# A graph-attention layer on one NeuronCore: rows led by their own column take x from the residual's tile instead of from the gather, blocks 4 to 23

## The chip, the cores and the metric

One core of a Trainium2 chip. The metric is device microseconds of one execution, the median of the runs. A profile is one execution, recorded by the hardware profiler; its span runs from the first to the last instruction.

## The reference

```
ht    = (h @ W) per head                 # h = x: 4096 x 512, W: 512 x (4 x 512)
e     = leaky_relu(src_i + dst_j) + adj  # adj: 4096 x 4096
att   = softmax(e, axis=-1)
gnn   = mean over heads of att @ ht
out   = layernorm(x + gnn, axis=-1)
```

Entries of `adj` are zero or random up to 1e9, and every diagonal entry is non-zero. A row's largest entry exceeds the next one so far that the softmax is one at that column and zero elsewhere. For such a row the layer is: find the column of the row's maximum, take that row of x, multiply it by the mean of the heads' weights, add the row's own x, normalise. The kernel does this, bounds the gap between the two largest entries, and has a general path (`general`) for rows where the bound fails; the data never need it.

In this data the row's own diagonal entry is the largest in 325 of 4,096 rows; in blocks 4 to 23 in 204 of 2,560.

## The kernel before, in words

The 4,096 rows are cut into 32 blocks of 128. Row p·32 + ib of the matrices belongs to block ib and sits in partition p. `leading_rows` is one loop over steps t = 0 to 31 (L432) with a tail behind it. The whole runs under a manual schedule (L55): each engine executes its instructions in the order in which the code emits them, and waits where an operand is not ready.

A block travels through the loop over several steps:

- SyncE's queue loads the block's 2 MB of `adj` five steps ahead (`load_adj`, L119), into six buffers in turn. x comes in larger pieces into `hold`, a tile that keeps all 32 blocks' x and later their outputs (`load_x`, L126; the table `x_at`, L427, says at which step which blocks). The second half of `hold` first holds the weights.
- Step t = ib: VectorE takes maxima over short segments of each row (`segment_maxima`, L180), the largest of them and its place (`find_segment`, L187 and L189). GpSimd computes the segment's number (L196) and fetches just that segment of each row by an indirect DMA (`fetch_segment`, L200, tile `lead`), then the segment's first column (L207, `start`).
- Step ib + 2: VectorE finds the place within the segment (L223, `within`), GpSimd adds it to `start` (L225, `col`) and gathers 128 rows of x by an indirect DMA into a tile `y` (`gather_rows`, L211; four buffers).
- Step ib + 3: TensorE turns y (L238), ScalarE copies the turned rows to SBUF (L240, `yt`), TensorE adds the block's own x through a product with the identity (`residual`, L246) and the four products with the mean weights (L253).
- Step ib + 4: ScalarE takes sum and squares of the result (`stats`, L275 and L277) and the norm of the block's own x (`row_norm`, L260).
- Every even step from 6: GpSimd turns two blocks' sums into factors (`rstd`, L280 to L282) and ScalarE, at the end of that step, writes the two blocks' outputs into `hold` (`finish`, L286). These are the blocks t - 6 and t - 5.

So in step t ScalarE's list is: the copy of one turned piece of W (steps 1 to 14), the copy of the turned rows of block t - 3, stats and row norm of block t - 4, and in even steps the two finishes. GpSimd's list is: column and gather of block t - 2, in even steps the statistics, then row, fetch and start of block t. The column is found between the two halves of step t's maxima on VectorE.

Until step 15 TensorE also turns W and forms the heads' vectors. Blocks 24 to 31 go a slightly different way, with the own x added later; the outputs are stored at the end, behind all loads in SyncE's queue.

Of the kernel before, what the change touches and what calls it, by code (L numbers as in the profile page):

```python
# [9 lines left out]
F32 = mybir.dt.float32  # L10
U32 = mybir.dt.uint32
I32 = mybir.dt.int32
AF = mybir.ActivationFunctionType
OP = mybir.AluOpType
# [6 lines left out]
P = 128  # L21
# [3 lines left out]
E_LAST = 64  # L25
EARLY = 18
LAST = 4


@with_exitstack  # L30
def gat_resnorm_kernel(
# [29 lines left out]
    any_bad = keep.tile([1, 1], I32, name="any_bad")  # L61

    leading_rows(tc, x, adj, W, a, out, ident, v, n_bad, any_bad)

    flag = nc.values_load(any_bad[0:1, 0:1], min_val=0, max_val=N)
# [5 lines left out]
def leading_rows(ctx, tc, x, adj, W, a, out, ident, v, n_bad, any_bad):  # L71
# [8 lines left out]
    nc = tc.nc  # L80
    N, D = x.shape
    H = a.shape[0]
    KB, NB = D // P, N // P
    AHEAD = 5
    Q = 4
# [4 lines left out]
    once = ctx.enter_context(tc.tile_pool(name="once", bufs=1))  # L90
    adj_pool = ctx.enter_context(tc.tile_pool(name="adj_pool", bufs=AHEAD + 1))
    y_pool = ctx.enter_context(tc.tile_pool(name="y_pool", bufs=4))
    lead_pool = ctx.enter_context(tc.tile_pool(name="lead_pool", bufs=1))
    LEADS = (8, 8, LAST)
    small = ctx.enter_context(tc.tile_pool(name="small", bufs=5))
# [3 lines left out]
    adj_rows = adj.rearrange("(p nb) m -> nb p m", nb=NB)  # L99
    spans = ((E_EARLY, 0, EARLY), (E, EARLY, NB - LAST), (E_LAST, NB - LAST, NB))  # L100
    adj_segs = {e: adj.rearrange("n (s e) -> (n s) e", e=e) for e, _, _ in spans}
# [6 lines left out]
    hold = once.tile([P, NB, D], F32, name="hold")  # L108
# [48 lines left out]
    nc.gpsimd.memset(power, -0.5)  # L157
    eps = once.tile([P, 1], F32, name="eps")
    nc.gpsimd.memset(eps, EPS)

    top = once.tile([P, NB, 8], F32, name="top")
    inner = once.tile([P, NB, 8], F32, name="inner")
# [45 lines left out]

    def gather_rows(ib, col):
        y = y_t[ib] = y_pool.tile([P, D], F32, name="y")  # L210
        nc.gpsimd.indirect_dma_start(  # L211
            out=y, out_offset=None, in_=x,
            in_offset=bass.IndirectOffsetOnAxis(ap=col[:, :1], axis=0),
        )
# [4 lines left out]
    def find_column(ib):  # L219
        if ib < BEHIND:  # L220
            find_inner(ib)
        within = small.tile([P, 8], U32, name="within")
        nc.vector.max_index(within, top[:, ib, :], lead_of[ib])  # L223
        col = small.tile([P, 1], U32, name="col")
        nc.gpsimd.tensor_tensor(col, at_of.pop(ib), within[:, 0:1], op=OP.add)  # L225
        gather_rows(ib, col)

    def find_column_in_row(ib):

        col = small.tile([P, 8], U32, name="col")  # L230
        nc.vector.max_index(col, top[:, ib, :], adj_t[ib])
        gather_rows(ib, col)
# [191 lines left out]
        nc.vector.tensor_reduce(total, pg, axis=AX.X, op=OP.add)  # L424
        nc.vector.tensor_scalar(any_bad, total, -1.0, float(N), op0=OP.mult, op1=OP.add)

    x_at = {Q - 1: (Q, 2 * Q), 3 * Q - 1: (3 * Q, Q), 4 * Q - 1: (4 * Q, 2 * Q)}  # L427
    vectors = [(kb, h) for kb in range(KB) for h in range(H)]
    vectors_at = {t: 2 if t < 3 else 1 for t in range(1, 15)}
    COLUMN, PROJECT, STATS, FINISH = 2, 3, 4, 6  # L430
# [1 line left out]
    for t in range(NB):  # L432
# [29 lines left out]
        ib = t - PROJECT  # L462
# [244 lines left out]
```

## Time and profile before

| | |
|---|---|
| median of 3 runs | 235.18 us (234.89 to 349.29) |
| span of the profiled execution | 233.4 us |
| TensorE, VectorE, ScalarE, GpSimd busy | 86%, 82%, 48%, 43% |
| moved by DMA | 97.12 MB, mean 416 GB/s |
| of which by GpSimd's queue (segments and gathered rows) | 8.84 MB |
| gathers of x | 32, 0.96 us each on GpSimd |

The span stands 1.8 us under the median; what lies around it is not in the profile. PE is TensorE's matmuls, PEld its weight loads, DVE is VectorE, ACT ScalarE, POOL GpSimd, SP SyncE. A row of the timeline has the start, the duration, the engine, the line of the kernel, the operation, the tiles (out<-in), and in brackets the idle time before it with what ended it. A row of the groups has the busy time, the mean of one in ns, and the idle time before. A row of the waits has the total, the number of times and the longest.

### The profile page before, as it was taken

The numbers are of one execution on the slowest core, as the hardware profiler recorded it, in microseconds if no ns is written. First come the engines' busy times: TensorE is split into PE (matmuls) and PEld (weight loads), VectorE is DVE, ScalarE is ACT, GpSimd is POOL, SyncE is SP. The second block draws the span as 40 slices with busy tenths as digits, with TensorE's granted clock in tenths as the row PEclk, the third lists the DMA queues.
The fourth block names the chain that finished last, engine by engine and source line by source line (L and its number), as shares of the span: only waits on it lengthen the run. The fifth ranks groups of instructions, "written<-read, shape, count | busy, mean of one in ns | idle before, by whom it ended". The sixth has DMA issues, their size and how long they took to land.

```text
span 233.4 us, 2484 instructions
## 1 busy us (share of the span) xinstructions
PE 199.9 (86%) x683; PEld 105.3 (45%) x683; DVE 191.3 (82%) x300; ACT 111.8 (48%) x267; POOL 100.7 (43%) x215
## 2 busy tenths in 40 slices
PE   0069995999999999999999779879998977999980
PEld 0034644646565555665645244334443433444460
DVE  0548299689929999999788995999999999998881
ACT  2001223014474757575767455545664644188561
POOL 2020234414524464644543452647464564548300
PEclk9999999579999999999999979999999999999997
DMA  6999999999999999999999999999999999999995
GB/s 237 423 432 428 428 438 426 415 439 436 422 421 437 423 431 425 431 419 428 430 430 428 432 423 432 423 430 421 426 433 420 426 423 426 412 424 420 421 414 213
DMA packets 12257, 97.12 MB, mean 416 GB/s; under 512 B 1992, under 2 KB 2440, under 8 KB 6480
## 3 DMA queue, kind: packets, MB, share of 16 engines
q1 hardware_dynamic: 8640, 88.08, 89.1%
q0 software_dynamic: 3584, 8.84, 9.6%
q8 instruction: 6, 0.10, 0.2%
q14 instruction: 11, 0.09, 0.1%
q10 hardware_dynamic: 16, 0.02, 0.0%
HBM read 88.54 MB, written 8.39 MB: 415 GB/s over the span
## 4 chain that ended last, share of the span: by engine, by line
DMA 64%; DVE 21%; PE 11%; SPq 1%; issue 1%; ACT 0%; DVEq 0%
DMA adj_t<-in_adj_dram 53%; DVE seg L180 17%; DMA hold<-in_x_dram 11%; PE o L253 6%; PE o L295 2%; DVE at L189 1%; PE tp L238 1%; DVE top L187 1%; PE o L246 1%; DVE within L223 1%; SPq L130 1%; PE o L291 0%; SPq L124 0%; DVE inner L217 0%; ACT hold L335 0%
## 5 line engine op out<-in xcount | busy, mean ns | idle before, releaser
L180 DVE TENSOR_REDUCE seg<-adj_t 128x128 f32<-128x2048 f32 (+3 forms) x66 | 145.5, 2208 | 28.5 <-DMA adj_t<-in_adj_dram 28.2
L253 PE MATMUL o<-w_sum,yt 128*128 128x512 f32 x248 | 117.6, 616 | 0.7 <-ACT yt L240 0.7
L253 PEld LDWEIGHTS o<-w_sum,yt 128*128 128x128 f32 x248 | 45.6, 196 | 55.2 <-issue 43.9
L240 ACT COPY yt<-tp 128x512 f32<-128x512 f32 x32 | 18.8, 588 | 43.9 <-PE tp L238 43.8
L200 POOL DMA_INDIRECT lead<-in_adj_dram,row x32 | 32.3, 1008 | 14.6 <-POOL row L196 14.6
L211 POOL DMA_INDIRECT y<-in_x_dram,col x32 | 30.9, 964 | 15.4 <-POOL col L225 15.1
L238 PE MATMUL tp<-ident,y 128*128 128x128 f32 x128 | 22.1, 296 | 10.2 <-DMA y<-in_x_dram,col 10.1
L246 PE MATMUL o<-hold,ident 128*128 128x512 f32 x52 | 28.5, 634 | 1.7 <-DMA hold<-in_x_dram 1.7
L343 PE MATMUL o<-hold,ident 128*128 128x512 f32 x32 | 17.3, 696 | 13.6 <-DMA hold<-in_L_gnn_W_dram 13.6
L238 PEld LDWEIGHTS tp<-ident,y 128*128 128x128 f32 x128 | 18.5, 209 | 22.8 <-issue 20.5
L361 ACT COPY wt<-tp 128x512 f32<-128x512 f32 x16 | 9.2, 587 | 38.2 <-PE tp L359 38.2
L196 POOL TENSOR_TENSOR row<-at,first 128x1 uint32<-128x1 uint32 x32 | 6.1, 190 | 43.6 <-DVE at L189 43.6
L367 PEld LDWEIGHTS pv<-at_d,wt 128*128 128x128 f32 x128 | 17.2, 200 | 7.4 <-ACT wt L361 3.7
L260 ACT ACTIVATE sq<-hold 128x512 f32<-128x512 f32 x32 | 19.8, 620 | 0.0
L225 POOL TENSOR_TENSOR col<-start,within 128x1 uint32<-128x1 uint32 x31 | 5.9, 190 | 32.2 <-DVE within L223 32.2
L286 ACT ACTIVATE hold<-o,nm,sd 128x512 f32<-128x512 f32 x24 | 17.2, 771 | 0.0
L277 ACT ACTIVATE sq<-o,nm 128x512 f32<-128x512 f32 x24 | 16.5, 687 | 0.8
L343 PEld LDWEIGHTS o<-hold,ident 128*128 128x128 f32 x32 | 6.9, 225 | 21.5 <-issue 21.5
L367 PE MATMUL pv<-at_d,wt 128*128 128x2 f32 x128 | 16.0, 249 | 0.6 <-ACT wt L361 0.6
L344 ACT ACTIVATE w_sum<-o 128x512 f32<-128x512 f32 x4 | 2.4, 598 | 27.5 <-PE o L343 27.5
L275 ACT ACTIVATE sq<-o 128x512 f32<-128x512 f32 x24 | 14.5, 606 | 0.0
L187 DVE MAX8 top<-seg 128x8 f32<-128x256 f32 (+2 forms) x32 | 11.6, 362 | 1.1
(86 smaller groups left out, 140.0 us busy)
## 6 DMA issues: line engine op xcount, KB each, us to landing
adj_t<-in_adj_dram SPq DMA_DIRECT2D x28, 2048.0 KB, 30.8
adj_t<-in_adj_dram SPq DMA_DIRECT2D x6, 1024.0 KB, 28.1
hold<-in_L_gnn_W_dram SPq DMA_DIRECT2D x2, 2048.0 KB, 16.4
hold<-in_x_dram SPq DMA_DIRECT2D x2, 2048.0 KB, 37.6
out_dram<-hold SPq DMA_DIRECT2D x4, 1024.0 KB, 16.1
out_dram<-hold SPq DMA_DIRECT2D x7, 512.0 KB, 14.4
hold<-in_x_dram SPq DMA_DIRECT2D x3, 1024.0 KB
adj_t<-in_adj_dram SPq DMA_DIRECT2D x4, 512.0 KB, 19.8
```

What stands on the lines that cost most here:

```text
L180: nc.vector.tensor_reduce(seg_of[ib][:, ts(k, N // e // n)], adj_t[ib][:, ts(k, N // n)].rearrange("p (s e) -> p s e", e=e), axis=AX.X, op ...
L200: nc.gpsimd.indirect_dma_start(out=lead, out_offset=None, in_=adj_segs[e], in_offset=bass.IndirectOffsetOnAxis(ap=row[:, :1], axis=0),)
L211: nc.gpsimd.indirect_dma_start(out=y, out_offset=None, in_=x, in_offset=bass.IndirectOffsetOnAxis(ap=col[:, :1], axis=0),)
L238: nc.tensor.transpose(tp[:, kb, :], y[:, ds(kb, P, KB)], ident)
L240: nc.scalar.copy(yt, tp)
L246: nc.tensor.matmul(o_ps[ib], ident, hold[:, ib, :], start=start, stop=False)
L253: nc.tensor.matmul(o_ps[ib], yt_of[ib][:, kb, :], w_sum[:, kb, :], start=(start and kb == 0), stop=(kb == KB - 1),)
L260: nc.scalar.activation(sq, hold[:, ib, :], AF.Square, accum_out=xx[:, ib : ib + 1])
L277: nc.scalar.activation(sq, o, AF.Square, bias=nm[:, i], accum_out=sd[:, i])
L286: nc.scalar.activation(hold[:, ib, :], o_ps.pop(ib), AF.Identity, bias=nm[:, i], scale=sd[:, i])
L343: nc.tensor.matmul(o, ident, hold[:, w_at + kb * H + h, :], start=(h == 0), stop=(h == H - 1))
L367: nc.tensor.matmul(pv[:, kb, h : 2 * H : H], wt[:, k, :], at_d[:, k, h : 2 * H : H], start=(k == 0), stop=(k == KB - 1),)
```

## The change

For blocks 4 to 23, GpSimd computes three more things from the column of each row: `same` (1 where the column is the row's own number, else 0), `away` (8192 there, else 0), and `there`, their sum with the column. ScalarE writes the block's own x, from `hold`, times `same` into the tile y: own rows where they lead, zeros elsewhere. The gather then runs with `there`: an index beyond the last row is skipped, so those rows of y keep what ScalarE wrote, and the others are overwritten. Since ScalarE now needs the block's x at step ib + 2 instead of TensorE at step ib + 3, three x loads are moved two steps forward.

```diff
+SKIP = 8192
+OWN = range(4, 24)
...
+    numbers = once.tile([P, NB], I32, name="numbers")
+    nc.gpsimd.iota(numbers, pattern=[[1, NB]], base=0, channel_multiplier=NB)
+    own = once.tile([P, NB], F32, name="own")
+    nc.gpsimd.tensor_copy(own, numbers)
...
     def gather_rows(ib, col):
         y = y_t[ib] = y_pool.tile([P, D], F32, name="y")
+        if ib in OWN:
+            same = small.tile([P, 1], F32, name="same")
+            nc.gpsimd.tensor_scalar(same, col, own[:, ib : ib + 1], None, op0=OP.is_equal)
+            away = small.tile([P, 1], U32, name="away")
+            nc.gpsimd.tensor_scalar(
+                away, col, own[:, ib : ib + 1], float(SKIP), op0=OP.is_equal, op1=OP.mult
+            )
+            there = small.tile([P, 1], U32, name="there")
+            nc.gpsimd.tensor_tensor(there, col, away, op=OP.add)
+            nc.scalar.activation(y, hold[:, ib, :], AF.Copy, scale=same)
+            nc.gpsimd.indirect_dma_start(
+                out=y, out_offset=None, in_=x,
+                in_offset=bass.IndirectOffsetOnAxis(ap=there[:, :1], axis=0),
+                bounds_check=N - 1, oob_is_err=False,
+            )
+            return
...
-    x_at = {Q - 1: (Q, 2 * Q), 3 * Q - 1: (3 * Q, Q), 4 * Q - 1: (4 * Q, 2 * Q)}
+    x_at = {1: (Q, 2 * Q), 3 * Q - 3: (3 * Q, Q), 4 * Q - 3: (4 * Q, 2 * Q)}
```

Q is 4: the pieces for blocks 4 to 11, 12 to 15 and 16 to 23 are loaded in steps 1, 9 and 13 instead of 3, 11 and 15, each ahead of that step's load of `adj`.

## The prediction

> **What bounds the kernel now.** I read the page first (shares, slices, queues, chain), then the waits, then the timeline of one block.
>
> ```profile
> span 233.4 us, 2484 instructions
> ...
> PE 199.9 (86%) x683; PEld 105.3 (45%) x683; DVE 191.3 (82%) x300; ACT 111.8 (48%) x267; POOL 100.7 (43%) x215
> ...
> DMA  6999999999999999999999999999999999999995
> ...
> DMA packets 12257, 97.12 MB, mean 416 GB/s; under 512 B 1992, under 2 KB 2440, under 8 KB 6480
> ...
> DMA 64%; DVE 21%; PE 11%; SPq 1%; issue 1%; ACT 0%; DVEq 0%
> ```
>
> The DMA engines are full from the second slice to the last but one, and 64% of the chain is DMA: 97.12 MB at 416 GB/s fill the span. But VectorE (82%) and TensorE (86%) stand close behind, so a delay on either that lasts to the last blocks ends in the time. Who waits:
>
> ```profile
> DVE seg L180 <- DMA adj_t<-in_adj_dram: 28.2, 11, 8.7
> ...
> PE tp L238 <- DMA y<-in_x_dram,col: 10.1, 10, 2.7
> ...
> L211 POOL DMA_INDIRECT y<-in_x_dram,col x32: 962/962/969, 31.1 to 214.6; - x32
> ...
> DMA to landing us min/median/max: 6.2/7.8/9.5
> ```
>
> TensorE waits ten times for gathered rows: there, y arrives just as PE wants it. The gather that the change edits takes 7.8 us (median) from issue to landing. It has no slack in the second half of the stage, and I look at one block of it. Counted from the first issue at 31.1 us, the gather at 162.78 below is block 21's, the turn at 159.71 block 19's, the turn at 170.67 block 21's.
>
> ```profile
> 158.38 0.19 POOL L280 TENSOR_SCALAR sd<-sd 128x2 f32<-128x2 f32 x1
> 158.66 0.72 POOL L281 TENSOR_TENSOR sd<-sd,power 128x2 f32<-128x2 f32 x1
> ...
> 159.71 0.72 PE L238 MATMUL tp<-ident,y 128*128 128x128 f32 x4
> ...
> 160.47 0.59 ACT L240 COPY yt<-tp 128x512 f32<-128x512 f32 x1 [2.49 <-PE tp L238]
> 160.95 0.60 ACT L275 ACTIVATE sq<-o 128x512 f32<-128x512 f32 x1
> ...
> 161.78 0.19 DVE L223 FIND_INDEX8 within<-top,lead 128x8 uint32<-128x32 f32 x1
> ...
> 162.05 0.19 POOL L225 TENSOR_TENSOR col<-start,within 128x1 uint32<-128x1 uint32 x1 [0.42 <-DVE within L223]
> ...
> 162.78 0.97 POOL L211 DMA_INDIRECT y<-in_x_dram,col  x1 [0.54 <-POOL col L225]
> ...
> 162.97 1.43 ACT L286 ACTIVATE hold<-o,nm,sd 128x512 f32<-128x512 f32 x2
> ...
> 165.29 0.72 PE L238 MATMUL tp<-ident,y 128*128 128x128 f32 x4 [0.49 <-DMA y<-in_x_dram,col]
> ...
> 168.46 0.19 ACT L260 ACTIVATION_READ_ACCUMULATOR sq<-hold 128x1 f32 x1
> ...
> 170.67 0.72 PE L238 MATMUL tp<-ident,y 128*128 128x128 f32 x4 [0.28 <-DMA y<-in_x_dram,col]
> ```
>
> Today the gather of block 21 needs only VectorE (within, then col). It is issued while ScalarE is still in the work of loop step 22: the copy of block 19's turned rows, stats and row norm of block 18, two finishes. Gather and ScalarE do not know of each other. Issue to landing to turn is 162.78 + 7.8 + 0.1 = 170.67.
>
> **The change, part by part.** *Bytes.* In the reference's data 204 of the 2,560 rows of blocks 4 to 23 are led by their own column. At 2 KB each that is 0.42 MB of 97.12 MB, at 416 GB/s 1.0 us of DMA work. It counts only if the DMA still sets the end.
>
> *Set-up.* One iota and one copy of 128x32 on GpSimd before any gather: two short instructions, like the 0.19 us ones above, while GpSimd has nothing due until the first maxima. Nothing; without that cover some 0.4 us.
>
> *Three GpSimd operations a block* (same, away, there), 128x1 each. The pair at 158.38 and 158.66 gives 0.28 us from one start to the next, so 0.84 us: the gather could go at 162.24 + 0.84 + 0.54 = 163.62. They lie inside the wait told next; without it they cost 0.84 us a block.
>
> *The x loads, two steps earlier.* The same 2, 1 and 2 MB pass two adjacency loads each in SP's queue. Their cost today is seen as a wait of VectorE:
>
> ```profile
> 69.15 2.29 DVE L180 TENSOR_REDUCE seg<-adj_t 128x128 f32<-128x2048 f32 x1 [4.03 <-DMA adj_t<-in_adj_dram]
> ```
>
> That wait comes two steps sooner. The bytes do not grow, and x is there when ScalarE wants it, since the distance to the need stays the same. Zero; if it fell on a gather without slack, at most those 4.0 us once.
>
> *The write of y by ScalarE, and the wait for it.* This is the dear part. The order on each engine is the order of emission. The write stands at the head of step t on ScalarE, behind everything of step t-1; for block 21 behind the finishes, which end at 162.97 + 1.43 = 164.40. The write itself is not in this trace. Nearest rows:
>
> ```profile
> L286 ACT ACTIVATE hold<-adj_t,nm,sd 128x512 f32<-128x512 f32 x4 | 3.1, 805 | 0.0
> ...
> L275 ACT ACTIVATE sq<-adj_t 128x512 f32<-128x512 f32 x3 | 1.9, 627 | 0.0
> ```
>
> Between 0.63 (fixed scale) and 0.81 us (scale and bias per partition, same memory); with one per-partition operand I take 0.72. GpSimd then issues the gather between 0.1 us (the step from engine to engine: within ends at 161.97, col starts at 162.05) and 0.54 us (its gap ahead of a gather) later; I take 0.3, as part of that gap can pass during the wait. The gather goes at 164.40 + 0.72 + 0.30 = 165.42, not 162.78. It lands 7.8 us later, and PE turns block 21 at 173.35 instead of 170.67.
>
> ScalarE's own wait for same costs nothing here: same is known near 162.24 + 0.28, before ScalarE gets there. Were it ahead, the copy of the next turned rows, for which TensorE waits, would queue behind.
>
> The late gather alone would be a shift of 2.7 us. But **it closes a ring**: turn of b-2, its copy, ScalarE's work behind that, write of y(b), gather, landing, turn of b. One round is 4.69 (159.71 to 164.40) + 0.72 + 0.30 + 7.8 + 0.13 = 13.64 us for two blocks. For an even b there are no finishes ahead: 168.46 + 0.19 - 165.29 = 3.36 in place of 4.69, a round of 12.3. TensorE takes blocks in order, so the odd ring sets 13.64 for two: 6.8 us a block. Now it is 5.5 here (159.71 to 165.29 to 170.67). The ring starts with block 3, whose gather is untouched, and its last gather with the write is that of block 23:
>
> ```profile
> 63.30 0.65 PE L238 MATMUL tp<-ident,y 128*128 128x128 f32 x4
> ...
> 181.90 0.72 PE L238 MATMUL tp<-ident,y 128*128 128x128 f32 x4 [0.45 <-DMA y<-in_x_dram,col]
> ```
>
> Ten rounds, blocks 3, 5, ... 23: 63.30 + 136.4 = 199.7 against 181.90, **17.8 us late on TensorE**. Bounds: 0.1 or 0.54 for the hand-over give 15.8 or 20.2; a landing of 8.2 and 0.54 some 24; one of 6.2, the shortest in the trace, 1.8.
>
> *Behind the waiting gather* on GpSimd stand the step's statistics and the next segment's fetch, so VectorE gets its segments late too:
>
> ```profile
> 176.35 0.19 POOL L196 TENSOR_TENSOR row<-at,first 128x1 uint32<-128x1 uint32 x1 [1.29 <-DVE at L189]
> 177.05 0.96 POOL L200 DMA_INDIRECT lead<-in_adj_dram,row  x1 [0.51 <-POOL row L196]
> ...
> 183.88 0.18 DVE L223 FIND_INDEX8 within<-top,lead 128x8 uint32<-128x32 f32 x1
> ...
> DMA to landing us min/median/max: 5.2/6.1/7.9
> ```
>
> Block 25's segment is fetched after block 23's gather: 199.7 - 7.9 = 191.8, plus 0.97 and 0.70 (row to fetch), 193.5, landing 6.1 later at 199.6, for a search that now runs at 183.88: **15.7 us late on VectorE**. Can the rest of the program win it back? What is left to wait for after 182 us:
>
> ```profile
> PE tp L238 <- DMA y<-in_x_dram,col: 2.3, 3, 1.3
> ...
> DVE seg L180 <- DMA adj_t<-in_adj_dram: 0.4, 2, 0.2
> ```
>
> VectorE has 0.4 us to give and TensorE 2.3, so VectorE ends about 15.3 and TensorE at least 15.5 late. I take 15.5. The 1.0 us of bytes is not credited: the DMA would run dry before the end.
>
> *Sum.* The span of 233.4 us lies 1.8 us under the median of 235.18 us. 233.4 + 15.5 + 1.8 = 250.7 us.
>
> **A rule against this.** The Trainium skill (DMA: Bandwidth & Descriptors, section Anatomy of one DMA — SWDGE (gpsimd) path) fits a transfer from this queue as 2.0 us plus its bytes at 436 GB/s, an estimate of 2.6 us for a gather of 256 KB. The trace does not agree: 7.8 us at the median, 6.2 at the least, with the engines full. By the rule a round would be 8.4 us, no lag would gather, and the sum would be 1.0 us under today.
>
> **The rivals.** *Short flight (the other side).* With 8% of the rows gone, and the DMA less full as the ring slows the loads, the landing could come sooner. The ring stops mattering when a round fits two blocks at their mean pace, (181.90 - 63.30) / 10 = 11.9 us, so from a landing of 7.8 - (13.64 - 11.9) = 6.0 us down. Then only the bytes are left: 235.2 - 1.0 = 234.2 us. Against it: no gather of the trace landed under 6.2 us, and the adjacency loads keep the engines full until the lag has eaten their queue. The rule above falls under this case.
>
> *A shift, not a round.* If lateness did not feed back, the end moves by one delay, 2.7 us at most: 237.9 us. For it: y has slack in the first half, where TensorE waits less. Against it: ScalarE's work ahead of the write starts with a copy that needs the turn two blocks before.
>
> *Starved loads.* If segment fetches land behind the gathers in the one software queue (8.2 us where 7.8 was taken, with 0.54 for the hand-over), VectorE lags some 24 us, its tiles come free late, and the load queue runs dry: 259 us.
>
> *The skipped rows still move.* If an index past the bound still costs a packet, the 1.0 us is not saved. Since it was not credited, the time stays 251 us; the DMA bytes tell.
>
> **How the numbers follow.** Forecast, ring with a lag near 15.5 us: 0.69, own range 244 to 257. Short flight 0.08, shift 0.07, starved loads 0.08, rows still moving 0.05, and 0.03 for a gain that I see no case for. Within 2% (4.7 us, about what a measurement of this kernel can tell from no change) are short flight and shift: 0.15. Slower are the forecast, starved loads and moving rows: 0.82. Faster: 0.03. The range leaves out the two mild cases and reaches down to a ring with landings of some 6.5 us, 63.30 + 123.4 - 181.90 = 4.8 late, 240; up to the starved case, 259.
>
> **What would show it.** A new group of 20 ScalarE writes of y near 0.72 us. GpSimd's gather idle before it, released by that write and not by col, 2 to 3 us after col in the early blocks of the stage. Turns two blocks apart by 13 to 14 us in blocks 5 to 23, ScalarE never waiting long there; waits of the segment search for lead where now there is 0.2 us; DMA slices under 9 after some 190 us. DMA bytes lower by 0.42 MB. I am wrong if the turns keep 11 to 12 us per pair: then either the landings got shorter than 6.5 us or ScalarE reaches the write before the column is known. If the gathers are late but the end is not, then TensorE or VectorE had room that the waits do not show.

## The result, and the profile after

The changed kernel takes 256.69 us (median of 4 runs, 255.66 to 257.2) against 235.09 us before: a ratio of 1.0915, 95% interval 1.0887 to 1.0943, so 21.6 us slower. The 235.09 us are the median of four runs, one more than in the table above, and one of them, at 349.29 us, was a slow run that the ratio leaves out. The forecast was 250.7 us in a range of 240 to 259. The profiled run of the changed kernel took 257.2 us with a span of 255.6.

The page of the changed kernel, its shares, slices and chain:

```profile
span 255.6 us, 2625 instructions
...
PE 209.1 (82%) x683; PEld 109.3 (43%) x683; DVE 191.7 (75%) x300; ACT 125.0 (49%) x287; POOL 118.9 (47%) x277
...
PEclk9999996599976999977999997999999979999999
DMA  6999999999999999999999999998999999971225
GB/s 255 427 434 427 435 419 430 434 425 438 419 431 428 426 422 440 423 435 422 433 424 433 424 431 424 407 389 348 374 352 407 410 320 417 424 288 53 78 110 225
...
DMA 45%; PE 32%; ACT 14%; issue 5%; POOL 1%; DVE 0%; SPq 0%; POOLq 0%
```

VectorE does the same work (191.7 us, 191.3 before) in a longer span. The DMA is no longer full to the end: its rate falls from slice 26 on, and in the last four slices its engines are busy for one to five tenths of the time. ScalarE, which had no share of the chain, now has 14%. 96.72 MB were moved instead of 97.12, and GpSimd's queue alone moved 8.42 instead of 8.84: the skip does what it says. The waits of the changed kernel:

```profile
POOL y L227 <- ACT y L226: 43.0, 18, 5.4
...
PE tp L260 <- DMA y<-in_x_dram,there: 23.0, 14, 3.8
DVE inner L239 <- DMA lead<-in_adj_dram,row: 22.8, 13, 3.2
```

The first line is new: 18 of the 20 gathers are put down as waiting for ScalarE's write of y, 43 us in all. TensorE's wait for y has more than doubled (10.1 us before), and VectorE, which hardly waited for segments (0.2 us), waits 22.8 us for them. The new groups of instructions:

```profile
L226 ACT ACTIVATE y<-hold,same 128x512 f32<-128x512 f32 x20 | 14.4, 719 | 2.3 <-POOL same L219 2.2
...
L227 POOL DMA_INDIRECT y<-in_x_dram,there x20 | 22.4, 1121 | 45.0 <-ACT y L226 43.0 <-PE tp L381 2.0
```

ScalarE itself waits only 2.2 us for `same`. It is late, not held up. One round of the ring, blocks 19 to 21, in the timeline:

```profile
180.12 0.72 PE L260 MATMUL tp<-ident,y 128*128 128x128 f32 x4 [1.16 <-DMA y<-in_x_dram,there]
...
180.88 0.59 ACT L262 COPY yt<-tp 128x512 f32<-128x512 f32 x1 [3.04 <-PE tp L260]
...
183.38 1.44 ACT L308 ACTIVATE hold<-o,nm,sd 128x512 f32<-128x512 f32 x2
...
183.81 0.19 POOL L225 TENSOR_TENSOR there<-col,away 128x1 uint32<-128x1 uint32 x1
...
184.71 0.72 ACT L226 ACTIVATE y<-hold,same 128x512 f32<-128x512 f32 x1
...
186.21 1.12 POOL L227 DMA_INDIRECT y<-in_x_dram,there  x1 [2.20 <-ACT y L226]
...
187.83 0.97 POOL L206 DMA_INDIRECT lead<-in_adj_dram,row  x1 [0.27 <-POOL row L202]
...
193.15 0.72 PE L260 MATMUL tp<-ident,y 128*128 128x128 f32 x4 [1.88 <-DMA y<-in_x_dram,there]
```

The rows to gather are known at 184.00 (`there`). ScalarE copies block 19's turned rows, does its other work, finishes two blocks until 184.82, and only then writes y. The gather follows 0.78 us behind the write (185.43 to 186.21), the segment fetch behind the gather, and TensorE turns block 21 at 193.15, 13.03 us after block 19. The ends of the ring:

```profile
63.27 0.53 PE L260 MATMUL tp<-ident,y 128*128 128x128 f32 x3
...
206.12 0.60 PE L260 MATMUL tp<-ident,y 128*128 128x128 f32 x3 [2.30 <-DMA y<-in_x_dram,there]
...
206.52 0.19 DVE L245 FIND_INDEX8 within<-top,lead 128x8 uint32<-128x32 f32 x1
```

Block 23 is turned at 206.12 instead of 181.90, 24.2 us late; VectorE searches block 25's segment at 206.52 instead of 183.88, 22.6 us late; the span ends 22.2 us late.

### The profile page after: what moved, and what is told of

Its sections match the earlier page's. It is cut to its first block, busy times and chain, and to the rows that moved or that the text cites. A ratio compares the mean times of both kernels' runs of the same rounds, so it can differ in the third digit from the quotient of the medians.

```text
span 255.6 us, 2625 instructions
## 1 busy us (share of the span) xinstructions
PE 209.1 (82%) x683; PEld 109.3 (43%) x683; DVE 191.7 (75%) x300; ACT 125.0 (49%) x287; POOL 118.9 (47%) x277
## 2 busy tenths in 40 slices
DMA packets 12259, 96.72 MB, mean 378 GB/s; under 512 B 2000, under 2 KB 2448, under 8 KB 6480
## 3 DMA queue, kind: packets, MB, share of 16 engines
q0 software_dynamic: 3584, 8.42, 9.2%
## 4 chain that ended last, share of the span: by engine, by line
DMA 45%; PE 32%; ACT 14%; issue 5%; POOL 1%; DVE 0%; SPq 0%; POOLq 0%
DMA y<-in_x_dram,there 27%; PE o L275 19%; DMA hold<-in_x_dram 12%; PE tp L260 4%; ACT hold L308 4%; PE o L268 3%; DMA y<-in_x_dram,col 3%; DMA adj_t<-in_adj_dram 3%; PE pv L389 3%; ACT sq L297 2%; ACT yt L262 2%; ACT y L226 2%; ACT sq L282 2%; PE o L317 1%; PE tp L381 1%
## 5 line engine op out<-in xcount | busy, mean ns | idle before, releaser
L275 PE MATMUL o<-w_sum,yt 128*128 128x512 f32 x248 | 123.8, 643 | 0.7 <-ACT yt L262 0.7
L275 PEld LDWEIGHTS o<-w_sum,yt 128*128 128x128 f32 x248 | 48.2, 206 | 59.6 <-issue 48.8
L227 POOL DMA_INDIRECT y<-in_x_dram,there x20 | 22.4, 1121 | 45.0 <-ACT y L226 43.0
L268 PE MATMUL o<-hold,ident 128*128 128x512 f32 x52 | 29.6, 658 | 1.5 <-DMA hold<-in_x_dram 1.5
L365 PE MATMUL o<-hold,ident 128*128 128x512 f32 x32 | 17.3, 697 | 13.5 <-DMA hold<-in_L_gnn_W_dram 13.5
L239 DVE MAX8 inner<-lead 128x8 f32<-128x16 f32 (+2 forms) x32 | 5.3, 183 | 23.0 <-DMA lead<-in_adj_dram,row 22.8
L389 PEld LDWEIGHTS pv<-at_d,wt 128*128 128x128 f32 x128 | 18.9, 217 | 7.7 <-issue 5.2
L389 PE MATMUL pv<-at_d,wt 128*128 128x2 f32 x128 | 17.5, 261 | 0.6 <-ACT wt L383 0.6
L226 ACT ACTIVATE y<-hold,same 128x512 f32<-128x512 f32 x20 | 14.4, 719 | 2.3 <-POOL same L219 2.2
```

The source lines that it names most:

```text
L226: nc.scalar.activation(y, hold[:, ib, :], AF.Copy, scale=same)
L227: nc.gpsimd.indirect_dma_start(out=y, out_offset=None, in_=x, in_offset=bass.IndirectOffsetOnAxis(ap=there[:, :1], axis=0), bounds_check=N ...
L268: nc.tensor.matmul(o_ps[ib], ident, hold[:, ib, :], start=start, stop=False)
L275: nc.tensor.matmul(o_ps[ib], yt_of[ib][:, kb, :], w_sum[:, kb, :], start=(start and kb == 0), stop=(kb == KB - 1),)
L365: nc.tensor.matmul(o, ident, hold[:, w_at + kb * H + h, :], start=(h == 0), stop=(h == H - 1))
L389: nc.tensor.matmul(pv[:, kb, h : 2 * H : H], wt[:, k, :], at_d[:, k, h : 2 * H : H], start=(k == 0), stop=(k == KB - 1),)
```

## The experiments

The theory: the write of y stands on ScalarE behind the work of the step before, that work needs the turn of two blocks before, and so lateness comes round again (the ring). The rivals: the added work itself, the bounded gather, the moved loads, ScalarE's wait for `same`.

**The skip taken away, the write and the wait kept.**

```diff
-                in_offset=bass.IndirectOffsetOnAxis(ap=there[:, :1], axis=0),
-                bounds_check=N - 1, oob_is_err=False,
+                in_offset=bass.IndirectOffsetOnAxis(ap=col[:, :1], axis=0),
```

> Changed kernel, but the gather takes the plain column and no bound, so that every row is fetched again over what ScalarE wrote; the write and the wait for it stay. Ring theory (the write of y stands behind the work of the step before, and that work needs the turn two blocks before): the wait stays, so 255 to 258 us, two-block pitch of the turns still near 13.8 us; the 0.4 MB that come back are not on the path. Rival, the bounded gather itself (skipped indices, the longer issue of 1.12 us) is what costs: most of the 21.6 us goes, below 245 us.

254.62 us, ratio 1.0833 [1.0815, 1.0851], 0.4 us under the lower end for the ring. Nearly all of the loss is there without a skipped row. The gather follows the write sooner than in the changed kernel:

```profile
170.15 1.06 POOL L227 DMA_INDIRECT y<-in_x_dram,col  x1 [3.22 <-ACT y L226]
```

ScalarE's write before it ends at 169.87, so the hand-over takes 0.28 us here and 0.78 us in the changed kernel. Between wait and issue the bounded gather has one register move and one more semaphore instruction on GpSimd's sequencer. The 2.1 us that this kernel gains on the changed one do not follow from the shorter hand-over alone: from block 5 to block 23 (78.47 to 203.99) its nine rounds take 13.95 us each, against 13.80 in the changed kernel. What it gains it gains before, in a first round of 14.3 us (64.13 to 78.47) instead of 18.6.

**The write one step earlier and without `same`.** Since the gather overwrites every row that is not skipped, the block's own x can be copied in for all rows, before the column is known.

```diff
+    def own_rows(ib):
+        y = y_t[ib] = y_pool.tile([P, D], F32, name="y")
+        nc.scalar.copy(y, hold[:, ib, :])
...
-            nc.scalar.activation(y, hold[:, ib, :], AF.Copy, scale=same)
...
         if t >= COLUMN:
             find_column(t - COLUMN)
+        if t - 1 in OWN:
+            own_rows(t - 1)
```

> Changed kernel, but ScalarE copies the block's own x into y for all rows, one step earlier and without the factor same (the gather overwrites the rows that are not skipped, so the result is the same). Skip, bound, away, there and the x loads stay. Ring theory: the gather waits for GpSimd alone, the turns go back to 11 to 12 us per two blocks, 233.5 to 237 us. Rival, the operations on GpSimd, the bounded gather or ScalarE's added 14 us are what costs: still above 245 us.

237.7 us, ratio 1.0098 [1.0074, 1.0121]. 19 of the 21.6 us are gone with the same skip, the same moved loads and nearly the same work on ScalarE (122.0 us busy instead of 125.0). GpSimd has one short operation a block less (`same`). The bounded gathers of this kernel:

```profile
L230 POOL DMA_INDIRECT y<-in_x_dram,there x20 | 22.2, 1112 | 13.8 <-ACT sq L302 4.8
```

Their idle time falls from 45.0 to 13.8 us, some 0.7 us before each (the name behind it is only what signalled last), and the turns of blocks 3 to 23 (63.85 to 185.91) are 12.2 us apart for two blocks, against 14.3 in the changed kernel (63.27 to 206.12). The place of the write in ScalarE's order is what cost the 19 us. The time is 0.7 us above what the ring led to expect, and what remains over the kernel before is followed up below.

**The x loads alone**, in the kernel before.

```diff
-    x_at = {Q - 1: (Q, 2 * Q), 3 * Q - 1: (3 * Q, Q), 4 * Q - 1: (4 * Q, 2 * Q)}
+    x_at = {1: (Q, 2 * Q), 3 * Q - 3: (3 * Q, Q), 4 * Q - 3: (4 * Q, 2 * Q)}
```

> Kernel before with the three x loads moved two steps forward and nothing else. Ring theory: the waits for adjacency move two steps, 235 us plus or minus 1. Rival, the loads in front of the adjacency tiles start the lag: 239 us or more (the wait of 4 us falls on a gather without slack).

235.24 us, ratio 1.0018 [0.9997, 1.0039]: no cost of its own.

**A plain copy at the same place**, so that ScalarE no longer waits for GpSimd.

```diff
-            nc.scalar.activation(y, hold[:, ib, :], AF.Copy, scale=same)
+            nc.scalar.copy(y, hold[:, ib, :])
```

> Changed kernel with a plain copy of the block's own x into y in place of the product with same, at the same place in ScalarE's order; so ScalarE's write no longer waits for GpSimd, but still stands behind the work of the step before. Ring theory: position is what counts, 0.1 us less in each of ten rounds, 253 to 257 us. Rival, the wait for same (ScalarE idle at the head of a step until the column is known, with the copies of the turned rows behind it) is what costs: 235 to 242 us.

255.06 us, ratio 1.0838 [1.082, 1.0856]. The wait for `same`, and GpSimd's operation that makes it, are worth at most 1.6 us; the place in ScalarE's order costs nearly all.

**The finishes behind the write**: the same work, with the 1.45 us of the two finishes out of the odd round.

```diff
         if t >= COLUMN:
             find_column(t - COLUMN)
+        if behind is not None:
+            finish(behind - FINISH)
+            finish(behind - FINISH + 1)
+            behind = None
...
         if pair:
-            finish(t - FINISH)
-            finish(t - FINISH + 1)
+            behind = t
```

> Changed kernel with each pair of finishes moved from the end of an even step to the next step, right behind the write of y; the work is the same. Ring theory: the odd round loses the 1.45 us of the finishes, from 13.8 to some 12.4 to 12.9 us in nine or ten rounds, so 9 to 14 us less: 243 to 249 us. Rival, the amount of added work on ScalarE and GpSimd is what costs, whatever its order: 255 to 258 us.

249.4 us, ratio 1.0607 [1.0582, 1.0632]: 7.3 us less for a mere change of order, so the amount of work is not the cause. It is 0.4 us above the upper end of what the ring was expected to give. The turns go from 64.11 to 197.49 us, 13.3 us a round and not 12.4 to 12.9. The rest went to the gather's flight. For the odd blocks 7 to 23, the step from the turn two blocks before to the end of ScalarE's write falls from 5.3 us on average in the changed kernel to 4.1, but the step from the gather's issue to the turn grows from 7.7 to 8.3. In this kernel the DMA moves over 400 GB/s in every slice from the second to the 36th; in the changed kernel it falls to between 320 and 374 in four slices from the 28th on.

**One more copy ahead of each write**, into a scratch tile.

```diff
+            nc.scalar.copy(rows.tile([P, D], F32, name="sq"), hold[:, ib, :])
             nc.scalar.activation(y, hold[:, ib, :], AF.Copy, scale=same)
```

> Changed kernel with one more ScalarE copy of 128x512 (into a scratch tile, never read) ahead of each write of y. Ring theory: each of the ten rounds grows by the copy's 0.5 to 0.6 us: 5 to 7 us more, 261 to 264 us. Rival, no feedback (the lag is the sum of fixed delays that later slack takes up, or the load on GpSimd sets the pace): 256 to 258 us.

259.42 us, ratio 1.1044 [1.0997, 1.1092]: 2.7 us more, above the rival's band and below the ring's. Ten rounds grew by 0.3 us each (63.45 to 209.31). Late in the stage gathers land sooner, block 21's turn 4.55 us after its gather's issue (189.91 to 194.46); in that stretch the DMA engines are 81% busy and move 333 GB/s. So the ring is there, but it is not rigid: the later it gets, the emptier the DMA and the shorter the flight. That the emptier DMA is the reason is argued from these rows, not tried by itself.

**GpSimd writes y in place of ScalarE**, so that the gather waits for GpSimd's list alone.

```diff
-            nc.scalar.activation(y, hold[:, ib, :], AF.Copy, scale=same)
+            nc.gpsimd.tensor_scalar(y, hold[:, ib, :], same, None, op0=OP.mult)
```

> Changed kernel with the product with same computed by GpSimd in place of ScalarE, so that the gather waits for nothing but GpSimd's own list. GpSimd works more (some 0.7 to 1.3 us a block), ScalarE less. Ring theory: no ring, only a later gather and later segment fetches; 238 to 244 us. Rival, work on GpSimd ahead of the gather is what costs: more work there, at least 255 us.

248.77 us, ratio 1.0566 [1.0536, 1.0597]. Better than the changed kernel, but 4.8 us above the upper end: a miss. The product takes 1.59 us, more than the 0.7 to 1.3 allowed for, and what it delays is the segment fetch. GpSimd's timeline in this kernel:

```profile
161.37 0.19 POOL L247 TENSOR_TENSOR col<-start,within 128x1 uint32<-128x1 uint32 x1
...
162.49 1.59 POOL L226 TENSOR_SCALAR y<-hold,same 128x512 f32<-128x512 f32 x1
164.36 1.12 POOL L227 DMA_INDIRECT y<-in_x_dram,there  x1 [0.28 <-POOL y L226]
...
165.98 0.99 POOL L206 DMA_INDIRECT lead<-in_adj_dram,row  x1 [0.27 <-POOL row L202]
```

The fetch of block 21's segment leaves at 165.98 and VectorE searches it for the column at 174.09, after waiting 1.72 us for it to land, 13.0 us after block 19's search at 161.10. From block 5 to block 21 (66.55 to 174.09) the searches are 13.4 us apart for two blocks. That is **a second ring**, through VectorE: column, GpSimd's list, gather, fetch, landing, column two blocks later. The prediction had only said that VectorE would follow.

**What is left of the early copy's cost.** Three kernels take it apart. The first drops `away`, `there` and the bound, so that blocks 4 to 23 reach the plain gather of the kernel before:

```diff
-            away = small.tile([P, 1], U32, name="away")
...
-            nc.gpsimd.tensor_tensor(there, col, away, op=OP.add)
...
-            nc.gpsimd.indirect_dma_start(
-                out=y, out_offset=None, in_=x,
-                in_offset=bass.IndirectOffsetOnAxis(ap=there[:, :1], axis=0),
-                bounds_check=N - 1, oob_is_err=False,
-            )
-            return
```

> The early copy without away, there and the bound: ScalarE's copy into y and the moved x loads stay, the gather takes the plain column and overwrites all. It tells what is left of the early copy's 2.3 us over the kernel before. If that is GpSimd's longer way from column to gather (two more operations, 1.11 instead of 0.96 us), with the segment fetch behind it: 234.8 to 235.8 us. If it is ScalarE's copies: 237 us or more.

235.11 us, ratio 0.9993 [0.9984, 1.0002]. Twenty more copies on ScalarE, placed early, cost nothing. The second keeps the two operations and drops only the bound:

```diff
-                in_offset=bass.IndirectOffsetOnAxis(ap=there[:, :1], axis=0),
-                bounds_check=N - 1, oob_is_err=False,
+                in_offset=bass.IndirectOffsetOnAxis(ap=col[:, :1], axis=0),
```

> The early copy with away and there computed as before, but the gather takes the plain column without a bound, so only the longer way on GpSimd is left. If the early copy's last 2.5 us come from that way (0.5 to 0.6 us more from column to gather, with the segment fetch landing behind the gather in the same queue): 236 to 237.5 us. If they come from the bounded gather itself (its longer issue, the skipping): 235 to 235.5 us.

238.18 us, ratio 1.0139 [1.0103, 1.0176], 0.7 us above the upper end. Two short operations on the way from column to gather (0.30 and 0.19 us) account for the whole rest: the gather of block 12 goes 1.41 us after its column's start here (108.14 to 109.55) and 0.73 us after it in the kernel before (162.05 to 162.78, block 21). The bound adds nothing visible to it here. The third moves the statistics behind the fetch:

```diff
-        if pair:
-            rstd(slice(t - FINISH, t - FINISH + 2))
...
         find_segment(t)
+        if pair:
+            rstd(slice(t - FINISH, t - FINISH + 2))
```

> The early copy with the skip, and the statistics of even steps moved on GpSimd behind the segment fetch, so that the fetch goes some 0.9 us sooner in even steps. If the early copy's last 2.3 us come from a second ring (column, GpSimd's list, segment fetch, landing, column two blocks later: 12.55 us in even steps where VectorE takes 11 to 11.3): 234.5 to 236 us. If they come from the later gather alone (turns late by the 0.8 us longer way from column to gather): no gain, 237 to 238 us.

238.76 us, ratio 1.0163 [1.0128, 1.0198]: no gain, 0.8 us above what was expected even then, and if anything a loss. The experiment is not a clean one. The statistics now stand ahead of the next step's column on GpSimd, and the columns of blocks 5, 7, 9 and 21 start 0.5 to 0.9 us after VectorE has found the place, instead of some 0.1 to 0.4 us with the early copy alone. The fetch also shares a queue with the gather issued before it, so that issuing it sooner need not let it land sooner. By the trace's landing times the fetch of block 13 in the kernel with the two operations lands at 114.92 and the gather of block 11 at 113.67; for blocks 19 and 17 it is 151.91 and 150.64; in the kernel before, for blocks 12 and 10, 105.29 and 104.02: 1.25 to 1.27 us behind each time. None of the 30 fetches that follow a gather in either kernel lands ahead of it; the median is 1.3 us behind, the least 0.4. So the second ring runs through the gather's landing, and what counts in it is the time from column to gather. The Trainium skill (DMA: Bandwidth & Descriptors, section Queues, rings and completion order) says, for the queues of SyncE and ScalarE, that each engine consumes a ring's descriptors in order but that a later one may finish its write before an earlier one; on GpSimd's queue, the landings here keep the order of issue. That the landing order is the whole reason is argued from these times, not tried.

**The skip in blocks 4 to 13 alone**, with the early copy.

```diff
-OWN = range(4, 24)
+OWN = range(4, 14)
```

> The early copy with the skip in blocks 4 to 13 alone, where the turns come several us after y has landed, so that a later gather should be covered there. Theory of GpSimd's longer way: the 1.4 us of lag gathered from block 14 on goes, 234.5 to 236 us, at best 0.5 us under the kernel before for the bytes. If the lag comes with the first blocks: 236.5 to 238 us.

235.3 us, ratio 1.0038 [1.0007, 1.0069], as expected: the loss is nearly gone, and there is no gain. The twelve runs do not lie evenly: seven took 234.8 to 235.4 us and five 237.3 to 237.9. No version with a skip beats the kernel before.

**Fewer gathered rows with nothing paid for them**: 112 of 128 rows in blocks 4 to 23, so the last 16 rows of y keep old contents and the output is not the layer's.

```diff
+        n = 112 if 4 <= ib < 24 else P
         nc.gpsimd.indirect_dma_start(
-            out=y, out_offset=None, in_=x,
-            in_offset=bass.IndirectOffsetOnAxis(ap=col[:, :1], axis=0),
+            out=y[:n], out_offset=None, in_=x,
+            in_offset=bass.IndirectOffsetOnAxis(ap=col[:n, :1], axis=0),
         )
```

> Kernel before, in which the gathers of blocks 4 to 23 fetch 112 rows instead of 128 and nothing else is added: it leaves out 16 rows a block, which keep what the buffer held, 0.66 MB in all. It asks what fewer gathered bytes are worth with nothing paid for them. If the DMA sets the end: 0.66 MB at 416 GB/s, 1.6 us less, 233.6 us (for the 0.42 MB of the change, 1.0 us). If VectorE and TensorE set the end as much as the DMA: 234.8 to 235.4 us.

247.51 us, ratio 1.0496 [1.0452, 1.054]: slower, which neither side expected. The stretches of this kernel, with the DMA's share and rate in the last two columns, and below them the two middle stretches of the kernel before:

```profile
30.00:55.00 25.00, 21.65 (x81) 12.95 (x80) 21.75 (x33) 6.04 (x13) 9.37 (x19) 0.79 1.01 418
60.00:120.00 60.00, 59.31 (x246) 34.78 (x245) 49.68 (x72) 35.80 (x86) 28.29 (x60) 1.00 1.01 377
130.00:190.00 60.00, 50.15 (x130) 22.87 (x130) 49.18 (x76) 30.05 (x74) 27.12 (x58) 0.89 1.01 383
200.00:235.00 35.00, 32.02 (x97) 14.54 (x96) 32.15 (x66) 20.22 (x51) 19.02 (x34) 1.00 1.02 422
...
60.00:120.00 60.00, 60.00 (x250) 35.34 (x249) 53.05 (x77) 36.11 (x88) 30.80 (x65) 1.00 1.01 428
130.00:190.00 60.00, 52.11 (x142) 23.38 (x141) 55.72 (x82) 33.23 (x84) 32.30 (x68) 0.97 1.01 426
```

While the 112-row gathers run the engines stay full and move 377 to 383 GB/s; with full gathers after them 422 (the kernel before: 428 and 426 in the two middle stretches). The profiled run is the slowest of six, 248.53 us, but the fastest took 244.72. So this kernel does not price the bytes; what the 0.42 MB are worth by themselves stays open. Why 112 rows slow everything was not tried.

## Why the prediction was right

The mechanism was right, step by step. *Wait:* 18 of 20 gathers are released by ScalarE's write, and ScalarE's own wait is small, as said. *The write:* 0.72 us taken, 0.719 measured. *ScalarE's work ahead of it:* 4.69 us taken, 180.12 to 184.82 gives 4.70. *The set-up and the moved loads:* no cost of their own (235.24 us with the loads alone, 235.11 with both and the early copies). *VectorE follows:* 22.6 us late, for the reason given. *The rest of the program gives little back:* 24.2 us at block 23 became 22.2 at the end. *The bytes:* 0.40 MB less, not credited, and rightly.

The lag itself was under-sized: 15.5 us forecast, 22.2 in the span. On TensorE block 23 is turned 6.4 us later than the 199.7 us of the sum. Three terms were off.

The **first round** holds 5.0 of these 6.4 us: 18.6 us, from 63.27 to block 5's turn at 81.89, instead of 13.64. Two things add up there. Block 4 is turned at 72.35 and not at 69.41. In the kernel with the moved loads alone, where VectorE's wait for adjacency falls on block 4's column as it does here, it is turned at 70.86: so about half of these 2.9 us come with the loads, which the prediction priced at zero or "at most those 4.0 us once", and the rest with the longer way from column to gather (61.32 to 63.47, where with the loads alone it is 61.22 to 61.95). The loads cost nothing without the ring. And TensorE then ran at half clock, told below, so that block 4 took it 9.5 us and not 6.1; the prediction has no term for that.

The **hand-over** from write to gather was the mis-sized term of the round. The prediction took 0.30 us "between 0.1 us ... and 0.54 us"; it is 0.78 us, outside both ends, with the bounded gather's additional instructions on GpSimd's sequencer after the wait. That is 0.48 us a round, 4.3 over the nine rounds from block 5 on.

The **landing** was taken as 7.8 us throughout. Turn follows issue by 8.85 us at block 9 (101.57 to 110.42) and by 6.94 at block 21. The bounded gathers of the changed kernel, of which the trace has the landing of five (blocks 7, 11, 15, 19 and 23):

```profile
L227 POOL DMA_INDIRECT y<-in_x_dram,there x20: 1119/1120/1131, 63.5 to 199.2; - x20
...
DMA to landing us min/median/max: 6.5/7.5/8.5
```

The landing goes above what was taken and ends below it (8.49 us at block 15, 6.48 at block 19), the short-flight rival setting in late, when the loads run low. The 2.6 us estimated from the Trainium skill's fit (DMA: Bandwidth & Descriptors, section Anatomy of one DMA — SWDGE (gpsimd) path) are not approached here either: the shortest of the five landings takes 6.48.

From block 5 on, nine rounds took (206.12 - 81.89) / 9 = 13.80 us against 13.64. That this agrees so well is partly luck: the first five took 14.64 us each (81.89 to 155.09) and the last four 12.76, outside the 13 to 14 that were to show it; and one of the five, to block 11's turn at 126.07, ended on TensorE behind a stretch at half clock and not on y. Over the nine, the hand-over added 4.3 us, the step from issue to turn took 1.8 less than in the sum, and ScalarE's part 1.1 less. The first experiment shows too that the terms do not simply add up: with 0.5 us less in the hand-over its rounds are no shorter.

Of the rivals, the shift without a round falls with the two-block pitch, rows that still move with the 0.40 MB. Starved loads at 259 us is nearer in time than the forecast (2.3 us off, the forecast 6.0) and half right in mechanism: fetches do land behind gathers and hold VectorE, 22.6 us late where that rival said some 24, though the DMA ran low only in the last part. The measured time lies 0.3 us inside the forecast's own range of 244 to 257 us.

## What to carry to other kernels

Before putting an instruction into an in-order engine's list, read which wait its predecessors there end on. If that wait depends on what the new instruction releases, two blocks earlier, the delay is no constant: it goes into the pace of the loop, and the row to compare it with is the pitch of the loop, not the instruction's 0.7 us. Take the sum of the round as an estimate: here 1.45 us out of it gave 0.9 us a round back, and one more copy cost 0.3, as the gathers' flight changed too. And an operand that every row may safely receive (here the own x, overwritten wherever the gather writes) needs no condition and can be written early; check that before computing a mask.

## What the runs showed of the hardware that was not expected

**The clock.** Behind the longer waits of TensorE its granted clock fell to half for a few us. Two stretches of the changed kernel, the clock in the third column from the end:

```profile
73.80:80.60 6.80, 6.80 (x16) 3.70 (x15) 6.11 (x9) 2.49 (x7) 3.58 (x9) 0.50 1.01 424
82.00:88.60 6.60, 6.60 (x32) 4.16 (x31) 4.10 (x8) 5.40 (x12) 1.08 (x3) 1.00 1.03 432
```

The first follows a wait of 2.81 us at 72.35: 16 matmuls in 6.8 us where the second has 32 in 6.6. Block 4 takes TensorE from 72.35 to 81.89, 9.5 us, where 6.1 is usual. The same came behind the waits of 2.48 us at 110.42 (block 9 took 9.55 us), 3.76 us at 155.09 and 2.30 us at 206.12; behind waits of up to 1.88 us it did not. In the kernel with one more copy it came behind a wait of 1.97 us and not behind one of 2.84, so these traces give no sharp limit. TensorE's busy time rose from 199.9 to 209.1 us for the same 683 matmuls. The Trainium skill (TensorE: Matmul & The Clock Gate, Part 1) has the clock fall after an idle window of about 3.4 us; here a wait of 2.30 us was enough.

**The gather's width.** With gathers of 112 rows instead of 128 the DMA engines were as full and 10 to 12% slower (377 to 383 GB/s against 428 and 426), for all that they moved meanwhile.
